# Expert rows gathered in channel quarters and turned on VectorE; copies of the last weights pinned in SP's queue

## The chip, the cores and the metric

One core of one Trainium2 chip runs the whole program. The metric is the device time of one execution in microseconds (us); for the kernel before it is the median of three runs. A profile is one further execution, taken by the hardware profiler.

The engines are called as the profile calls them: PE is TensorE (matrix products; PEld is its weight load), DVE is VectorE, ACT is ScalarE, POOL is GpSimd, and SP is SyncE, which here only issues transfers. Each engine works through its own queue in order and waits on semaphores for the others.

## The reference

The input is x of 4 rows (batches) x 512 tokens x 512 channels, in float32. Two layers are computed, each with a gate ahead of its mixer and a gate ahead of its feed-forward part:

```python
x = x + L0_attn(L0_cond(x, f, f, ...))    # a state-space mixer (Mamba-2)
x = x + L0_ffn(L0_cond2(x, f, f, ...))    # mixture of 8 experts, top 2
x = x + L1_attn(L1_cond(x, f, f, ...))    # causal attention, 16 heads, 4 key/value groups
x = x + L1_ffn(L1_cond2(x, f, f, ...))    # gated feed-forward part, 1408 wide
```

The part that the change touches is the mixture of experts:

```python
logits = x @ gate_w.T + gate_b
top_vals, top_idx = jax.lax.top_k(logits, 2)
routing = softmax(top_vals)
for e in range(8):
    h = x @ w1[e].T + b1[e]                     # 512 -> 1024
    x_glu, x_lin = h[:, 0::2], h[:, 1::2]
    y = x_glu * sigmoid(1.702 * x_glu) * (x_lin + 1.0)
    ye = y @ w2[e].T + b2[e]                    # 512 -> 512
    out = out + ye * sum(routing * (top_idx == e))
```

## The kernel before

**Stages.** The program is unrolled; its stages overlap where the data allow it. From the start to about 650 us the four rows go through the state-space mixer; from 654 to about 1130 us the expert blocks run, the first of them between the last tiles of the mixer; from about 1131 to 1985 us comes attention, 64 heads (4 groups x 4 rows x 4 heads); then the last feed-forward part. A generator (`make_gates`, L352) is advanced a step at a time inside all of these and makes the gates of later parts, mostly on VectorE and ScalarE, with transfers on SP's queue.

**Order of the work.** The source gives an order, and a planner lays every engine's instructions out in advance: among those that its model holds ready it takes the one that the source has first. So an instruction without a wait can stand much earlier in a queue than in the source. `after(*engines)` (L88) pins what is traced in it behind the last instruction that the source has given to those engines so far.

**The experts.** Each token goes to two of eight experts. The 4096 token places are sorted by expert into blocks of 128 (class `Experts`, L709). There are 39 block numbers; 37 (`ALWAYS`) are always run, the last two only where the routing needs them. The first 17 (`NEARLY`) hold tokens of the first three rows done and are ordered by a first routing table (`order_blocks(0, NEARLY)`, called at L1433); the other 22 by a second one (L1525), after the last row is routed. A table is made by small products on PE and small operations on VectorE (L648 to L707): `use` says which block numbers are in use, `rank` puts them in order (a product with the constant `tri_lt`, L663 or L672), `of` is the one-hot form of that order, and the products at L689 and L690 pick from `toks` the token places of every block and from `v_e` its expert. The results are `idx_h` (which row of `rows_h` each of the 128 lanes takes), `idx_o` (where its result goes) and `eb` (the expert).

`rows_h` lies in device memory, 2048 tokens x 512 channels. A block goes through these steps, one call of `round` (L864) per block, with three blocks in different steps at a time:

- `fetch` (L766): one indirect transfer from GpSimd's queue gathers 128 rows of 2 KB into `hb`, token by partition. It is asked for three blocks ahead; `hb` has three buffers.
- `flip` (L776): four 128x128 transposes on PE (L782) bring channels onto the partitions, and one copy on ScalarE (L784) takes the result from PSUM to `hT`, which has two buffers.
- `first_half` (L806): products with the two halves of w1 (L811 and L822, 4 products each, which the profile counts double), the bias and the gate on VectorE (L816, L826, L828, L829), the tanh on ScalarE. The result is `u`.
- `finish` (L832): four more transposes on PE (L835) and a scaled copy on ScalarE (L837) into `yT`.
- `down` (L840): products with w2 (L844), the bias on VectorE (L849), and an indirect transfer that scatters the rows into `rows_o` (L850).

The weights come over SP's queue (`load_w1` L742, `load_w2` L754) and are loaded only where the expert in the slot changes. From block 17 on there are two slots.

**Attention.** For each head, `scores` (L1626) makes the softmax, turns it in 32x32 blocks on VectorE (L1653, the operation that the change also uses), writes it to device memory from GpSimd's queue (L1661) and reads it back as `pT` on SP's queue (L1678, `collect`); `context` (L1682) multiplies it with the values (L1703), about a head later than the load is issued. Between the heads, SP's queue carries the gates' transfers (L240, L247, L249, L344) and group weights (L1466).

**Copies of the last weights.** `gateT`, `upT` and `downT` of the last feed-forward part are copied within device memory, 2816 KB each, by SP (L1763), to be loaded from there at L1834 to L1839. The source has these three transfers in attention, at the first heads of rows 0 to 2 of group 2, and they wait for nothing. In the profile they are issued at 51.0, 56.9 and 57.4 us.

Of the kernel before, what the change touches and what calls it, by code (L numbers as in the profile page):

```python
# [10 lines left out]
F32 = mybir.dt.float32  # L11
# [35 lines left out]
HPG = HEADS // GROUPS  # L47
SCALE = KVC ** -0.5
# [35 lines left out]
def block_kernel(ctx: ExitStack, tc: tile.TileContext, a: dict, out: bass.AP):  # L84
# [61 lines left out]
    def ps_tp(name):  # L146
        return ps.tile([P, 512], F32, tag="tp", name=name, bufs=2)
# [263 lines left out]
    def gated(l, b, xb, pool, part=slice(0, T), **kw):  # L411
# [25 lines left out]
    tri_lt = rt.tile([P, P], F32, name="tri_lt")  # L437
    nc.gpsimd.affine_select(out=tri_lt, in_=ones, compare_op=ALU.is_gt, fill=0.0, base=0,
                            pattern=[[1, P]], channel_multiplier=-1)

# [36 lines left out]
    v_lo = rt.tile([P, 1], F32, name="v_lo")  # L477
    v_e = rt.tile([P, 1], F32, name="v_e")
# [48 lines left out]
    def route(lg, b, fine, pool, **kw):  # L527
# [25 lines left out]
        nc.tensor.matmul(pc[:, :n], lhsT=tri_lt, rhs=mm_, start=True, stop=True)  # L553
# [89 lines left out]
    idx_h = rt.tile([P, NBLK], I32, name="idx_h")  # L643
# [4 lines left out]
    def order_blocks(lo, hi):  # L648

        n = hi - lo  # L650
        cv = rt.tile([P, 1], F32, tag="cv", name="cv")
# [10 lines left out]
        if lo == 0:  # L662
            nc.tensor.matmul(pi[:, P : P + 1], lhsT=tri_lt, rhs=use, start=True, stop=True)  # L663
            nc.vector.tensor_copy(rank, pi[:, P : P + 1])
        else:
# [6 lines left out]
            nc.tensor.matmul(pi[:, P : P + 2], lhsT=tri_lt, rhs=two, start=True, stop=True)  # L672
# [9 lines left out]
            )  # L682
        if lo == 0:
            nc.vector.scalar_tensor_tensor(taken, rank, float(n), use, ALU.is_lt, ALU.mult)
# [7 lines left out]
        gf = tmp.tile([P, NBLK], F32, tag="th", name="gf")  # L692
        nc.vector.tensor_scalar(gf[:, :n], pi[:, :n], NROW - 2.0, None, ALU.add)
        nc.vector.tensor_copy(idx_h[:, lo:hi], gf[:, :n])
        low = tmp.tile([P, NBLK], I32, tag="th", name="low")
        nc.vector.tensor_scalar(
            low[:, :n], idx_h[:, lo:hi], T - 1, (B - 1) * T, ALU.bitwise_and, ALU.bitwise_xor
        )
        nc.vector.tensor_scalar(
            idx_h[:, lo:hi], idx_h[:, lo:hi], 1, (B - 1) * T,  # L700
            ALU.logical_shift_right, ALU.bitwise_and,
        )
        nc.vector.tensor_tensor(idx_h[:, lo:hi], idx_h[:, lo:hi], low[:, :n], ALU.bitwise_xor)
# [5 lines left out]
    class Experts:  # L709
# [56 lines left out]
        def fetch(self, i):  # L766
            if i >= self.known or i in self.hb:
                return
            hb = self.sm.tile([P, C], F32, tag="hb", name="hb", bufs=3)
            nc.gpsimd.indirect_dma_start(  # L770
                out=hb, out_offset=None, in_=rows_h[: (B if i >= NEARLY else B - 1) * T, :],
# [1219 lines left out]
```

## Time and profile before

| what | value |
|---|---|
| runs | 2265.02, 2266.19 and 2270.69 us; median 2266.19 |
| the profiled execution's own time | 2262.92 us |
| its span, from the first to the last instruction | 2260.90 us |
| mean granted PE clock | 0.983 |
| busy: PE, PEld, DVE, ACT, POOL | 2123.0, 1219.8, 1524.8, 971.5, 418.4 us |
| DMA: bytes moved, mean rate | 357.38 MB, 158 GB/s |
| expert stage, 655 to 1130 us: PE, DVE, ACT, POOL busy | 452.2, 260.3, 141.7, 92.1 of 475 us |
| attention, 1131 to 1985 us: PE, DVE, ACT, POOL busy | 824.1, 574.7, 328.1, 136.0 of 854 us |

How to read the lines. A group of instructions is given by its source line, engine and operation, what it writes and reads (partitions x elements, type), how often, then busy us and the mean ns of one, then the idle time of the engine just ahead of it and what ended that. In an answer by time the first two columns are start and duration in us, and the brackets hold the idle time ahead. An answer by windows has, for each stretch, its length, the busy us of each engine (with the number of instructions), the granted PE clock, the busy share of the 16 DMA engines and their GB/s. Products on PE are pipelined, so their durations overlap; what one costs is read from start to start.

### The profile page before, as it was taken

What the parts mean: (1) busy time and instruction counts of PE and PEld (TensorE: products, weight loads), DVE (VectorE), ACT (ScalarE), POOL (GpSimd) and SP (SyncE); (2) the same over time, 40 slices, a digit from 0 to 9 for tenths busy, and PEclk for the clock granted to TensorE, in tenths of its full rate; (3) what the DMA queues carried; (4) which work ended last, traced back from release to release, by engine and by line L of the source; (5) the groups of instructions that cost most, each with busy time, mean ns of one, the idle gap of its engine ahead of it and who ended that gap; (6) DMA issues with size and microseconds to landing.
All of it is one profiled execution on the core that took longest, in us unless ns stands there. A gap on an engine that the chain in (4) does not pass through costs nothing.

```text
span 2260.9 us, 23897 instructions
## 1 busy us (share of the span) xinstructions
PE 2123.0 (94%) x7528; PEld 1219.8 (54%) x7528; DVE 1524.8 (67%) x3040; ACT 971.5 (43%) x1901; POOL 418.4 (19%) x558
## 2 busy tenths in 40 slices
PE   2879999999999999999989999999999999999998
PEld 1545565555655444444444555545555555568887
DVE  8698989989643665566577767677767765465332
ACT  4476676766732234333154433333334333243221
POOL 4023242321331111211211111111111111100000
PEclk9889999999999999999989999999999999999999
DMA  7542241531523548978666555455545464441100
GB/s 261 174 141 75 95 166 66 169 111 63 193 71 135 192 159 297 352 261 292 210 238 206 177 181 168 140 164 185 169 151 164 147 196 133 148 158 38 38 19 20
DMA packets 112455, 357.38 MB, mean 158 GB/s; under 512 B 14595, under 2 KB 23171, under 8 KB 102915
## 3 DMA queue, kind: packets, MB, share of 16 engines
q1 hardware_dynamic: 87584, 277.26, 36.1%
q0 software_dynamic: 22432, 74.34, 11.0%
q10 hardware_dynamic: 2304, 4.20, 0.5%
q8 instruction: 62, 1.02, 0.2%
q14 instruction: 73, 0.57, 0.1%
HBM read 337.91 MB, written 108.00 MB: 197 GB/s over the span
## 4 chain that ended last, share of the span: by engine, by line
PE 36%; DVE 9%; DMA 2%; ACT 2%; issue 1%; SPq 0%; DVEq 0%; ACTq 0%
PE pd L1718 9%; PE pq L1615 5%; PE pctx L1703 3%; PE psc L1637 3%; PE pk L1593 3%; PE pv L1601 3%; PE pfo L1821 2%; PE pfo L1820 2%; PE pfg L1820 2%; PE pfg L1821 2%; PE pfu L1821 2%; PE pfu L1820 2%; DVE turned L1653 2%; DVE nmax L1642 2%; DMA pT<-turned 1%; DVE pr L1649 1%
## 5 line engine op out<-in xcount | busy, mean ns | idle before, releaser
L1661 POOL DMA_DIRECT2D turned<-turned x248 | 135.2, 552 | 701.2 <-DVE turned L1653 399.0
L1615 PE MATMUL pq<-h,wq 128*128 128x512 f32 x512 | 230.9, 593 | 2.2 <-DVE h L404 1.7
L1718 PE MATMUL pd<-cx,wd 128*128 128x512 f32 x512 | 224.0, 593 | 1.9 <-ACT cx L1711 1.6
L128 ACT ACTIVATE pr<-psc,nmax 128x128 f32<-128x128 f32 (+3 forms) x256 | 134.6, 526 | 166.1 <-DVE nmax L1642 165.4
L1048 PE MATMUL pc<-h,wxb 128*128 128x512 f32 x320 | 148.5, 620 | 42.8 <-DVE h L1307 38.9
L1640 DVE TENSOR_TENSOR psc<-psc,mask 128x128 f32<-128x128 f32 x256 | 70.7, 284 | 144.3 <-PE psc L1637 144.3
L1637 PE MATMUL psc<-kT,qT 128*128 128x128 f32 (+3 forms) x512 | 156.3, 442 | 12.0 <-ACT pr L128 12.0
L1718 PEld LDWEIGHTS pd<-cx,wd 128*128 128x128 f32 x512 | 95.6, 190 | 118.5 <-issue 108.1
L1703 PE MATMUL pctx<-pT,v 128*128 128x512 f32 (+3 forms) x512 | 149.7, 434 | 9.9 <-DMA pT<-turned 9.6
L1703 PEld LDWEIGHTS pctx<-pT,v 128*128 128x128 f32 x512 | 96.6, 190 | 90.2 <-issue 61.1
L1615 PEld LDWEIGHTS pq<-h,wq 128*128 128x128 f32 x512 | 92.6, 190 | 96.3 <-issue 90.8
L811 PE MATMUL pg<-w,hT 128*128 128x512 f32 x296 | 136.6, 603 | 6.8 <-ACT hT L784 6.8
L844 PE MATMUL po<-w,yT 128*128 128x512 f32 x296 | 135.9, 600 | 6.2 <-ACT yT L837 6.2
L822 PE MATMUL pn<-w,hT 128*128 128x512 f32 x296 | 133.4, 593 | 0.0
L1048 PEld LDWEIGHTS pc<-h,wxb 128*128 128x128 f32 x320 | 61.9, 198 | 115.8 <-issue 73.8
L1642 DVE TENSOR_REDUCE nmax<-psc 128x1 f32<-128x128 f32 (+3 forms) x256 | 122.7, 482 | 2.1
L1637 PEld LDWEIGHTS psc<-kT,qT 128*128 128x128 f32 x512 | 85.9, 192 | 70.5 <-ACT pr L128 26.9
L1726 DVE TENSOR_TENSOR xr<-xr,pd 128x512 f32<-128x512 f32 x64 | 43.5, 680 | 117.7 <-PE pd L1718 117.7
L1653 DVE STREAM_TRANSPOSE turned<-pr 128x128 f32<-128x128 f32 x248 | 120.7, 498 | 1.8
L1119 PE MATMUL pz<-wzt,h 128*128 128x512 f32 x256 | 115.2, 599 | 0.3 <-ACT st L1220 0.3
L1267 PE MATMUL po<-wot,yT 128*128 128x512 f32 x256 | 114.2, 600 | 0.0
L811 PEld LDWEIGHTS pg<-w,hT 128*128 128x128 f32 x296 | 56.2, 194 | 75.9 <-issue 66.3
(343 smaller groups left out, 4172.9 us busy)
## 6 DMA issues: line engine op xcount, KB each, us to landing
w<-in_w1x SPq DMA_DIRECT2D x76, 1024.0 KB
turned<-turned POOLq DMA_DIRECT2D x248, 208.0 KB, 4.0
pT<-turned SPq DMA_DIRECT2D x62, 832.0 KB
w<-in_w2x SPq DMA_DIRECT2D x38, 1024.0 KB
wb<-in_b1x SPq DMA_DIRECT2D x38, 512.0 KB
lm<-cs SPq DMA_DIRECT2D x32, 512.0 KB
kt<-in_fT SPq DMA_DIRECT2D x62, 256.0 KB
ek<-ek SPq DMA_DIRECT2D x62, 256.0 KB
```

Source lines behind the costliest of these rows:

```text
L811: nc.tensor.matmul(pg, lhsT=hT[:, k, :], rhs=self.w1[s][0][:, k, :], start=(k == 0), stop=(k == NC - 1))
L844: nc.tensor.matmul(po, lhsT=yT[:, j, :], rhs=self.w2[s][:, j, :], start=(j == 0), stop=(j == NI - 1))
L1048: nc.tensor.matmul(pc, lhsT=wxb[:, k, m * P : (m + 1) * P], rhs=h[:, k, :], start=(k == 0), stop=(k == NC - 1),)
L1615: nc.tensor.matmul(pq, lhsT=u.wq[:, k, i * KVC : (i + 1) * KVC], rhs=u.h[:, k, :], start=(k == 0), stop=(k == NC - 1),)
L1637: nc.tensor.matmul(psc[:, :n], lhsT=qT[:, qi * P : n], rhs=u.kT[:, :n], start=True, stop=True)
L1642: nc.vector.tensor_reduce(nmax, psc[:, :n], AX.X, ALU.max, negate=True)
L1653: nc.vector.transpose(blocks[:, :, 3 * qi : 4 * qi + 1, :].rearrange("p c k j -> p k c j"), pr)
L1661: nc.gpsimd.dma_start(out=d[:, :, r].rearrange("c i s -> i c s"), in_=blocks[r * SQ : (r + 1) * SQ].rearrange("i c k j -> i c (k j)"),)
L1703: nc.tensor.matmul(pctx[:, kj * P :].rearrange("p (q r j) -> p q r j", r=QUAD, j=SQ), lhsT=u.v[:, kj, :], rhs=pT[:, :, 4 * kj : 10 + kj : ...
L1718: nc.tensor.matmul(po, lhsT=dense_w[u.g][:, i, m * P : (m + 1) * P], rhs=u.ctxT[i], start=(i == 0), stop=(i == HPG - 1),)
L1820: nc.tensor.matmul(out_, lhsT=w, rhs=xs[0], start=first_, stop=False)
L1821: nc.tensor.matmul(out_, lhsT=w, rhs=xs[1], start=False, stop=last_)
```

## The change

It has four parts.

1. **Gather by quarters.** `rows_h` is read as rows of 128 channels, four to a token. `idx_h` gets four columns per block. `fetch` issues four indirect transfers per block instead of one, each with 128 rows of 512 bytes. Partition 32q + i of part r takes channel quarter q of token 32r + i of the block.
2. **Turn on VectorE.** `flip` becomes one `nc.vector.transpose` of 128x512, which turns each 32x32 block; its output is `hT` with the channels in another order, and w1 is laid out to that order on the host (`by_quad`). PE's four transposes and ScalarE's copy are gone.
3. **The routing table.** In each `order_blocks` a tile `wide` (128x512, made from `toks` by one copy on VectorE) takes part in four more products with `of`; the index operations work on four times the columns, and one more combines in `quarter`, which is made there too, by an iota on GpSimd and an operation on VectorE. `tri_lt`, a constant made at the start, is gone: the counts use `tri_gt`, and the ranks `tri_le` with `use` subtracted.
4. **The copies.** The three transfers of L1763 are put into `after(nc.sync)`.

```diff
@@ -45,6 +45,8 @@
 
 HEADS, GROUPS, KVC = 16, 4, 128
 HPG = HEADS // GROUPS
+SQ = 32
+QUAD = P // SQ
 SCALE = KVC ** -0.5
 MASKED = -1.0e30
 
@@ -434,10 +436,6 @@
     nc.gpsimd.affine_select(out=before, in_=before, compare_op=ALU.is_gt, fill=0.0, base=0,
                             pattern=[[1, E], [-1, E]], channel_multiplier=0)
 
-    tri_lt = rt.tile([P, P], F32, name="tri_lt")
-    nc.gpsimd.affine_select(out=tri_lt, in_=ones, compare_op=ALU.is_gt, fill=0.0, base=0,
-                            pattern=[[1, P]], channel_multiplier=-1)
-
     sel = rt.tile([P, E], F32, name="sel")
     nc.gpsimd.affine_select(out=sel, in_=ones[:, :E], compare_op=ALU.is_ge, fill=0.0, base=0,
                             pattern=[[-NQ, E]], channel_multiplier=1)
@@ -474,8 +472,8 @@
     e_nq = count("e_nq", [[NQ, E]])
     v_id = count("v_id", [[1, 1]], 1)
 
-    v_lo = rt.tile([P, 1], F32, name="v_lo")
-    v_e = rt.tile([P, 1], F32, name="v_e")
+    v_both = rt.tile([P, 2], F32, name="v_both")
+    v_lo, v_e = v_both[:, 0:1], v_both[:, 1:2]
     jk = rt.tile([P, E], F32, name="jk")
     nc.vector.tensor_tensor(jk, sel, e_nq, ALU.mult)
     nc.vector.tensor_reduce(v_e, jk, AX.X, ALU.add)
@@ -550,7 +548,7 @@
             yield
         pc = ps_tp("pcnt")
         mm_ = m.rearrange("p t e -> p (t e)")
-        nc.tensor.matmul(pc[:, :n], lhsT=tri_lt, rhs=mm_, start=True, stop=True)
+        nc.tensor.matmul(pc[:, :n], lhsT=tri_gt, rhs=mm_, start=True, stop=True)
         nc.tensor.matmul(pc[:, n : 2 * n], lhsT=ones, rhs=mm_, start=True, stop=True)
         for t in range(NT):
             bt = b * NT + t
@@ -640,7 +638,8 @@
 
 
     taken = rt.tile([P, 1], F32, name="taken")
-    idx_h = rt.tile([P, NBLK], I32, name="idx_h")
+    idx_h = rt.tile([P, QUAD, NBLK], I32, name="idx_h")
+    quarter = rt.tile([P, 1], I32, name="quarter")
     idx_o = rt.tile([P, NBLK], I32, name="idx_o")
     eb = rt.tile([1, NBLK + 1], I32, name="eb")
     in_use = eb[:, NBLK:]
@@ -648,6 +647,12 @@
     def order_blocks(lo, hi):
 
         n = hi - lo
+        if lo == 0:
+            with after(nc.gpsimd, nc.vector):
+                nc.gpsimd.iota(quarter, pattern=[[1, 1]], base=0, channel_multiplier=1)
+                nc.vector.tensor_scalar(
+                    quarter, quarter, 5, QUAD * (B - 1) * T, ALU.logical_shift_right, ALU.bitwise_xor
+                )
         cv = rt.tile([P, 1], F32, tag="cv", name="cv")
         nc.vector.tensor_tensor(jk, sel, cnt[:, (N2 if lo else N2 - NT), :], ALU.mult)
         nc.vector.tensor_reduce(cv, jk, AX.X, ALU.add)
@@ -660,8 +665,8 @@
         pi = ps_tp("pidx")
         rank = rt.tile([P, 1], F32, tag="vrank", name="vrank")
         if lo == 0:
-            nc.tensor.matmul(pi[:, P : P + 1], lhsT=tri_lt, rhs=use, start=True, stop=True)
-            nc.vector.tensor_copy(rank, pi[:, P : P + 1])
+            nc.tensor.matmul(pi[:, P : P + 1], lhsT=tri_le, rhs=use, start=True, stop=True)
+            nc.vector.tensor_tensor(rank, pi[:, P : P + 1], use, ALU.subtract)
         else:
 
             two = rt.tile([P, 2], F32, tag="two", name="two")
@@ -669,7 +674,7 @@
             nc.vector.tensor_reduce(rank, jk, AX.X, ALU.add)
             nc.vector.tensor_scalar(two[:, 0:1], v_lo, rank, use, ALU.is_lt, ALU.mult)
             nc.vector.tensor_tensor(two[:, 1:2], use, two[:, 0:1], ALU.subtract)
-            nc.tensor.matmul(pi[:, P : P + 2], lhsT=tri_lt, rhs=two, start=True, stop=True)
+            nc.tensor.matmul(pi[:, P : P + 2], lhsT=tri_le, rhs=two, start=True, stop=True)
             nc.tensor.matmul(pi[:, P + 2 : P + 3], lhsT=ones, rhs=two[:, 0:1], start=True, stop=True)
             nc.tensor.matmul(pi[0:1, P + 3 : P + 4], lhsT=ones[:, 0:1], rhs=use, start=True, stop=True)
             nc.vector.tensor_copy(in_use, pi[0:1, P + 3 : P + 4])
@@ -680,6 +685,7 @@
             nc.vector.scalar_tensor_tensor(
                 rank, pi[:, P : P + 1], two[:, 0:1], rank, ALU.mult, ALU.add
             )
+            nc.vector.tensor_tensor(rank, rank, use, ALU.subtract)
         if lo == 0:
             nc.vector.scalar_tensor_tensor(taken, rank, float(n), use, ALU.is_lt, ALU.mult)
         of = tmp.tile([P, NBLK], F32, tag="th", name="of")
@@ -689,18 +695,36 @@
         nc.tensor.matmul(pi[:, :n], lhsT=toks, rhs=of[:, :n], start=True, stop=True)
         nc.tensor.matmul(pi[0:1, 2 * P : 2 * P + n], lhsT=v_e, rhs=of[:, :n], start=True, stop=True)
 
-        gf = tmp.tile([P, NBLK], F32, tag="th", name="gf")
-        nc.vector.tensor_scalar(gf[:, :n], pi[:, :n], NROW - 2.0, None, ALU.add)
-        nc.vector.tensor_copy(idx_h[:, lo:hi], gf[:, :n])
-        low = tmp.tile([P, NBLK], I32, tag="th", name="low")
+
+        wide = tmp.tile([P, QUAD, QUAD, SQ], F32, tag="th", name="wide")
+        nc.vector.tensor_copy(
+            wide,
+            toks.rearrange("p (r j) -> p r j", r=QUAD).unsqueeze(2).to_broadcast([P, QUAD, QUAD, SQ]),
+        )
+        for r in range(QUAD):
+            nc.tensor.matmul(
+                pi[:, 3 * P + r * n : 3 * P + (r + 1) * n],
+                lhsT=wide[:, r].rearrange("p q j -> p (q j)"),
+                rhs=of[:, :n], start=True, stop=True,
+            )
+        ih = idx_h[:, :, lo:hi]
+        gf = tmp.tile([P, QUAD, n], F32, tag="th", name="gf")
         nc.vector.tensor_scalar(
-            low[:, :n], idx_h[:, lo:hi], T - 1, (B - 1) * T, ALU.bitwise_and, ALU.bitwise_xor
+            gf, pi[:, 3 * P : 3 * P + QUAD * n].rearrange("p (r n) -> p r n", r=QUAD),
+            NROW - 2.0, None, ALU.add,
+        )
+        nc.vector.tensor_copy(ih, gf)
+        low = tmp.tile([P, QUAD, n], I32, tag="th", name="low")
+        nc.vector.tensor_scalar(
+            low, ih, 2, QUAD * (T - 1), ALU.logical_shift_left, ALU.bitwise_and
         )
         nc.vector.tensor_scalar(
-            idx_h[:, lo:hi], idx_h[:, lo:hi], 1, (B - 1) * T,
-            ALU.logical_shift_right, ALU.bitwise_and,
+            ih, ih, 1, QUAD * (B - 1) * T, ALU.logical_shift_left, ALU.bitwise_and
         )
-        nc.vector.tensor_tensor(idx_h[:, lo:hi], idx_h[:, lo:hi], low[:, :n], ALU.bitwise_xor)
+        nc.vector.tensor_tensor(ih, ih, low, ALU.bitwise_xor)
+        nc.vector.tensor_tensor(
+            ih, ih, quarter.unsqueeze(2).to_broadcast([P, QUAD, n]), ALU.bitwise_xor
+        )
         ef = tmp.tile([1, NBLK], F32, tag="th", name="ef")
         nc.vector.tensor_scalar(ef[:, :n], pi[0:1, 2 * P : 2 * P + n], E - 1.0, None, ALU.add)
         nc.vector.tensor_copy(eb[:, lo:hi], ef[:, :n])
@@ -766,22 +790,25 @@
         def fetch(self, i):
             if i >= self.known or i in self.hb:
                 return
-            hb = self.sm.tile([P, C], F32, tag="hb", name="hb", bufs=3)
-            nc.gpsimd.indirect_dma_start(
-                out=hb, out_offset=None, in_=rows_h[: (B if i >= NEARLY else B - 1) * T, :],
-                in_offset=bass.IndirectOffsetOnAxis(ap=idx_h[:, i : i + 1], axis=0),
-            )
+            hb = self.sm.tile([P, QUAD, NC * SQ], F32, tag="hb", name="hb", bufs=3)
+            quarters = rows_h[: (B if i >= NEARLY else B - 1) * T, :].rearrange(
+                "r (q c) -> (r q) c", q=QUAD
+            )
+            for r in range(QUAD):
+                nc.gpsimd.indirect_dma_start(
+                    out=hb[:, r, :], out_offset=None, in_=quarters,
+                    in_offset=bass.IndirectOffsetOnAxis(ap=idx_h[:, r, i : i + 1], axis=0),
+                )
             self.hb[i] = hb
 
         def flip(self, i):
             if i in self.hT or i not in self.hb:
                 return
             hb = self.hb[i]
-            pt = ps_tp("pfl")
-            for k in range(NC):
-                nc.tensor.transpose(pt[:, k * P : (k + 1) * P], hb[:, k * P : (k + 1) * P], ident)
             hT = self.sm.tile([P, NC, P], F32, tag="hT", name="hT", bufs=2)
-            nc.scalar.copy(hT.rearrange("p k t -> p (k t)"), pt)
+            nc.vector.transpose(
+                hT.rearrange("p k (r j) -> p r k j", r=QUAD), hb.rearrange("p r c -> p (r c)")
+            )
             self.hT[i] = hT
 
         def weights(self, i, early=False):
@@ -1568,8 +1595,7 @@
             )
             return wd
 
-        SQ, SLOTS = 32, 13
-        QUAD = P // SQ
+        SLOTS = 13
         turned = [mp.tile([P, QUAD, SLOTS, SQ], F32, name=f"turned{i}") for i in range(2)]
         for blocks in turned:
             for lo, hi in ((1, 3), (5, 6)):
@@ -1760,7 +1786,8 @@
                 combine(b + 1)
             if g == 2 and i == 0 and b < 3:
                 to, name = ((ffg_d, "gateT"), (ffu_d, "upT"), (ffd_d, "downT"))[b]
-                nc.sync.dma_start(out=to, in_=a[name])
+                with after(nc.sync):
+                    nc.sync.dma_start(out=to, in_=a[name])
             if g and b == 0 and i == 3:
                 dense_w[g] = load_dense(g)
             if n + 1 < len(heads_):
@@ -1949,7 +1976,8 @@
         "gate_b": n["L0_ffn_gate_b"],
     }
     by_part = lambda v: v.reshape(E, -1, P, v.shape[-1]).swapaxes(1, 2)
-    w1x = np.stack([by_part(t(w1[:, i::2, :])) for i in range(2)], 2)
+    by_quad = lambda v: v.reshape(E, QUAD, NC, SQ, -1).swapaxes(2, 3).reshape(E, P, NC, -1)
+    w1x = np.stack([by_quad(t(w1[:, i::2, :])) for i in range(2)], 2)
     got = {
         "cols": np.concatenate([cols[k] for k, _ in _COLS], 1),
         "rows": np.concatenate([np.asarray(rows[k]) for k, _ in _ROWS]),
```

## The prediction

> **What bounds the kernel now.** I read the engines' shares first, then the slices, then the stage that the change touches, and there the waits and the instructions in order of time.
>
> ```profile
> PE 2123.0 (94%) x7528; PEld 1219.8 (54%) x7528; DVE 1524.8 (67%) x3040; ACT 971.5 (43%) x1901; POOL 418.4 (19%) x558
> ...
> PE   2879999999999999999989999999999999999998
> ...
> DMA  7542241531523548978666555455545464441100
> ```
>
> TensorE is full from the fourth slice on, so an instruction taken off its queue is worth its whole duration unless something else is about to end last. The expert blocks run from 654 to 1130 us. There the answer by windows (columns: stretch, length, busy us of PE, PEld, DVE, ACT, POOL, granted clock, DMA share, GB/s) reads:
>
> ```profile
> 840.00:880.00 40.00, 37.96 (x110) 17.76 (x109) 24.90 (x31) 15.73 (x21) 6.06 (x6) 1.00 0.80 274
> ...
> 920.00:960.00 40.00, 36.72 (x100) 17.18 (x99) 20.94 (x29) 13.49 (x18) 7.03 (x6) 0.96 1.00 373
> ...
> 1000.00:1040.00 40.00, 38.66 (x115) 18.80 (x114) 28.00 (x34) 13.89 (x21) 7.90 (x7) 1.00 0.76 273
> 1040.00:1080.00 40.00, 40.00 (x114) 19.00 (x113) 26.04 (x32) 11.02 (x17) 6.25 (x6) 1.00 0.69 241
> ```
>
> PE has 37 to 40 of each 40 us, VectorE at most 28, GpSimd 8. Only the DMA engines come close, and fill one window (share 1.00). So PE bounds this stage, with the weight stream just behind it. VectorE, ScalarE and GpSimd have room.
>
> **Removed: the TensorE flip.** Each of 37 blocks has four transposes (L782) and one copy out of PSUM on ScalarE (L784); the groups give busy us, mean ns of one, and the idle time before them.
>
> ```profile
> L782 PE MATMUL pfl<-ident,hb 128*128 128x128 f32 x148 | 23.2, 281 | 3.0 <-DMA hb<-rows_h,idx_h 3.0
> ```
>
> ```profile
> L784 ACT COPY hT<-pfl 128x512 f32<-128x512 f32 x37 | 21.5, 581 | 40.1 <-PE pfl L782 40.1
> ```
>
> In order of time (start, duration, what):
>
> ```profile
> 741.05 0.60 PE L782 MATMUL pfl<-ident,hb 128*128 128x128 f32 x4
> 741.49 3.60 PE L822 MATMUL pn<-w,hT 128*128 128x512 f32 x8
> ```
>
> The rows overlap by pipelining, so the cost is from start to start: 741.49 - 741.05 = 0.44 us per block; other blocks read the same. The first two flips stand in the wait for the first gather and are counted there; the other 35 give 35 x 0.435 = **-15.2 us**.
>
> The copy on ScalarE costs only where PE waits for it: three waits of PE for hT, 6.8 us in all. The longest is 4.18 us at 800.6; the product behind it then took 6.01 instead of 3.60 us (granted clock 0.93 in 800 to 840), so 9.2 us hang on it. Without the copy that product starts at once, but the next transposes need u (L829), which ends at 802.5 because ScalarE's tanh is late too; it would gain only the half us that the copy held it up. So about 4.5 us of that stall go, and little of the others: **-5** (bounds -9.2 and 0).
>
> **Added per block: four gathers and a VectorE transpose.** A gather is 0.94 to 1.48 us on GpSimd, 1.27 from start to start:
>
> ```profile
> 654.05 1.24 POOL L770 DMA_INDIRECT hb<-rows_h,idx_h  x1 [7.32 <-DVE eb L706]
> 655.59 0.97 POOL L770 DMA_INDIRECT hb<-rows_h,idx_h  x1 [0.30 <-issue]
> 656.86 0.95 POOL L770 DMA_INDIRECT hb<-rows_h,idx_h  x1 [0.30 <-issue]
> ```
>
> Four take 5.1 us where one took 1.3; with the scatter of the results (1.3) GpSimd has 6.4 us of work in a round of 11 to 12 us. Block i+3 is asked for when block i is turned, over two rounds (22 us) ahead; 5.1 plus 4.5 us to landing (median) fit in. The bytes stay the same, but rows shrink from 2 KB to 512 B. The packet records have 28.9 ns for a 512-byte packet, and 187 ns for two 2 KB rows: per block 512 x 28.9 / 16 = 0.92 us of all engines instead of 64 x 187 / 16 = 0.75, some 0.2 us, hidden except where DMA is full.
>
> The transpose has an exact row, the attention's own:
>
> ```profile
> L1653 DVE STREAM_TRANSPOSE turned<-pr 128x512 f32<-128x512 f32 x62 | 43.7, 704 | 1.1
> ```
>
> 37 x 0.704 = 26 us on VectorE, 0.70 in a round that uses some 8 of 12 us. It waits for four gathers; queued behind it on VectorE are the bias additions, gates and scans, and PE's next transposes wait for u. PE waits for u 0.7 us in the whole stage now. I take **+1** (0 to +5).
>
> The Trainium skill has a rule against this ("SBUF — State Buffer", "SBUF: two separate sides"): while VectorE runs a two-port operation, GpSimd cannot write descriptors, and a transfer of 620 ns took 3100. By that, 148 gathers 2.5 us longer each would cost 370 us of GpSimd, more than the stage has left, and the gathers would set the pace. The trace shows gathers of at most 1.48 us beside a busy VectorE; it does show 128x1 operations on GpSimd (L1247) of 0.34 to, in the mean, 1.26 us. No gather row shows the rule's price.
>
> **First table (651 to 662 us), fully exposed.** PE now waits 2.71 us for the first gather and starts the first product at 661.94, after two flips and eight transposes of the mixer (L1258). After the change come `wide` (0.5 to 0.7; nearest rows L1649 and L404 at 128x512: 476 and 697 ns), four more pairs of products (0.22 each from start to start, by L689 to L690) and two more small VectorE operations (0.18), partly beside other work: indices 1.3 us later. The fourth gather starts 3 x 1.27 = 3.8 us after the first. The turn is 0.70 instead of 1.08 (PE) + 0.59 (ScalarE). First operand: 659.5 + 1.3 + 3.8 - 1.0 = 663.6, product at 663.7: +1.8. The clock was at half from 655 to 662 (a flip 1.08 instead of 0.60); if that lasts 3.4 us longer at half speed, one or two such pieces add 1.7 or 3.4. Bounds 0 and +5.2; **+3.5**. `quarter` falls into GpSimd's idle 7.3 us: nothing.
>
> **Second table (772 to 778 us).** Its blocks are due 80 us later, so only PE's queue counts: 4 x 0.22 = 0.9, and a short wait for `wide`, as PE waits 1.14 for `of` (L686) today: **+1.2** (0.9 to 1.6).
>
> **Weight stream.** Faster rounds ask for weights sooner. In the window at share 1.00 PE already waits 3.28 us, put down to yT, which had long been there. About four rounds cannot shrink, and the smaller rows add 0.2 each to a few more: **+2** (0 to +9: all 20 rounds from 840 to 1080).
>
> **The late copies.** Three transfers of 2816 KB between HBM tensors are issued at 51.0, 56.9 and 57.4 us and occupy the DMA engines until 82 (9.8 us each). At that time only one wait for a DMA shows (VectorE, 0.8 us), so their going gains 0 to 0.8. Behind the change each stands on SP's queue ahead of attention's loads of pT. The packet records give each load's landing; it lands 17 to 29 us before its use for two heads of four, 7 to 9 for the third, and about 0.5 to 3 for the fourth:
>
> ```profile
> 1594.98 0.37 SPq L1678 DMA_DIRECT2D pT<-turned  x1
> ```
>
> ```profile
> 1601.45 2.39 PE L1703 MATMUL pctx<-pT,v 128*128 128x512 f32 x8 [2.55 <-DMA pT<-turned]
> ```
>
> A copy straight before the third load costs PE 9.8 - 7.4 = 2.4 us, before the fourth 9.3, before the others nothing: -0.8 to +28 for the three. `after(nc.sync)` pins them behind the last gate or pT transfer of the previous head, mostly ahead of a load with room: **+2**.
>
> **Sum**: -15.2 - 5 + 1 + 3.5 + 1.2 + 2 + 2 = -10.5. The profiled execution took 2262.92 us (span 2260.90 and 2.02 around it): 2252.4. The median of the runs shown is 2266.19, 3.3 above it; forecast for the median: 2255.7, or **2256 us**. All favourable ends (-15.2 - 9.2 + 0.9 - 0.8 = -24.3) give 2242; the unfavourable ones, with copies at 7: -15.2 + 5 + 5.2 + 1.6 + 9 + 7 = +12.6, 2279.
>
> **Rivals.** *No gain, 2266*: the weight stream holds the 20 rounds from 840 to 1080 at their length (+8.7 instead of +2, no gain from the copy on ScalarE): -10.5 + 6.7 + 5 = +1.2. For it: DMA share 0.69 to 1.00 there, half of all blocks. Against: PE fills those windows, and share 1.00 occurs in one.
>
> *Slower, 2282*: the copies land on the fourth head's load, which has 0.5 us to spare (PE waits 2.55 there today): 3 x 9.3 = 28 us instead of 2, so -10.5 + 26 = +15. It eats the whole gain from 4.2 us per copy on. For it: SP's queue is in order and the transfers behind a copy wait. Against: only one load in four is that tight.
>
> *It does not do what it says*: the copies stay early; then 2254.
>
> **Chances.** Forecast 0.62 (faster 0.56, same 0.06), no gain 0.22 (0.04, 0.16, slower 0.02), slower 0.16 (0.13, same 0.03). Bounded by 0.3% (6.8 us, about what a measurement of this kernel can tell from no change): faster 0.60, same 0.25, slower 0.15. Range: from the favourable end, 2242, up to 2278, where most of the slower rival is left out.
>
> **What would show it.** Right: no L782 or L784 rows; 148 gathers of about 1 us; 37 transposes of 0.70; rounds 0.44 us shorter except in one window; the first product near 664; no waits of PE for pT beyond 3 us around 1560 to 1690. Wrong: gathers of 2 us or more, PE waiting for the transpose, or the copies in front of a tight pT load. I hold the order of all other instructions to be unchanged; since it is planned anew, stalls may move elsewhere, and that is the largest unknown.

## The result, and the profile after

The changed kernel takes 2286.43 us (median of 6 runs, 2282.31 to 2287.86) where the kernel before takes 2265.61 beside it: a ratio of 1.0079, interval 1.0063 to 1.0095. It is 20.8 us slower; the forecast's sum had it 10.5 faster. The profiled execution took 2287.86 us (span 2286.0, granted clock 0.974 instead of 0.983).

The page after, engines' shares and slices as before:

```profile
PE 2131.2 (93%) x7396; PEld 1216.1 (53%) x7396; DVE 1546.0 (68%) x3083; ACT 951.8 (42%) x1864; POOL 545.3 (24%) x669
...
PE   2879999999987999999989999999999999999998
...
DMA  6142341432513457987667555456845464431100
```

PE is busy 8 us longer than before, VectorE 21 and GpSimd 127. And PE's twelfth and thirteenth slices (629 to 743 us), full before, have fallen to 8 and 7. The windows (stretch, length, busy us of PE, PEld, DVE, ACT, POOL, granted clock, DMA share, GB/s) give the place, and two windows of the later blocks for comparison:

```profile
680.00:720.00 40.00, 26.94 (x64) 12.08 (x63) 8.85 (x15) 3.31 (x6) 19.91 (x27) 0.83 0.29 92
...
920.00:960.00 40.00, 40.00 (x103) 18.27 (x102) 28.60 (x38) 12.79 (x17) 19.56 (x19) 1.00 1.00 361
1000.00:1040.00 40.00, 37.77 (x98) 17.11 (x97) 27.68 (x37) 12.56 (x17) 21.64 (x18) 1.00 0.72 258
```

From 680 to 720 us PE is busy 26.9 us of 40, at a clock of 0.83, while GpSimd works 19.9. Further on PE has its 38 to 40 us again. The two new operations, by groups:

```profile
L809 DVE STREAM_TRANSPOSE hT<-hb 128x512 f32<-128x512 f32 x37 | 25.9, 701 | 10.1 <-DMA hb<-rows_h,idx_h 10.1
```

```profile
L798 POOL DMA_INDIRECT hb<-rows_h,idx_h x148 | 172.1, 1163 | 158.0 <-DVE hT L809 107.6 <-issue 35.0 <-DVE idx_h L725 8.2
```

The turn takes the forecast 0.70 us. A gather takes 1.16 us in the mean and 2.0 at most, so no gather row shows the price of 3100 ns that the prediction weighed.

**Round by round.** The interval from one block's first product (L811, now L838) to the next block's is the measure of the blocks. The table has the rounds that differ, for the kernels that are told of below; the last two rows are the sum of 36 intervals and the half-clock time within them.

| round | before | after | after again (e9) | one pin (e1) | gates pinned: changed (e14) | before (e16) | mixture (e15) |
|---|---|---|---|---|---|---|---|
| 0 | 7.7 | 10.3 | 9.5 | 9.2 | 10.3 | 7.8 | 9.2 |
| 1 | 18.6 | **33.4** | **33.2** | 18.6 | 18.6 | 18.6 | 18.6 |
| 8 | 13.2 | 18.0 | 17.9 | 14.6 | 18.0 | 13.2 | 14.3 |
| 9 | 15.5 | 10.7 | 10.7 | 10.7 | 10.7 | 11.2 | 11.2 |
| 10 | 13.6 | 16.5 | 16.4 | 17.8 | 16.0 | 12.4 | 12.4 |
| 14 | 12.2 | 15.8 | 16.9 | 15.8 | 15.8 | 13.2 | 11.7 |
| 22 to 24, each | 11.2 | 10.7 | 10.7 | 10.7 | 10.7 | 11.2 | 10.7 |
| 25 | 12.8 | 13.2 | 13.2 | 13.2 | 10.7 | 11.2 | 10.7 |
| 29 | 12.8 | 14.9 | 14.9 | 14.9 | 10.7 | 11.2 | 10.7 |
| all 36 | 448.4 | 460.8 | 459.4 | 445.0 | 434.7 | 432.5 | 425.8 |
| half clock | 10.2 | 39.2 | 37.6 | 19.9 | 18.7 | 0.2 | 3.0 |

So in the profiled run the blocks lost 12.4 us: 2.6 in the first round, 14.8 in the second, and five later rounds (8, 10, 14, 25, 29) got 13.9 longer; the other 29 got 18.9 shorter in sum. Two further losses lie outside the blocks: 9.0 us before the first table, and 4.4 in the last feed-forward part. The 9.0, 0.3 at the first table, the 12.4, about -0.9 from the last block to the last part and the 4.4 add up, within rounding, to the 25.1 between the spans.

**The second round.** PE in order of time:

```profile
671.28 6.19 PE L838 MATMUL pg<-w,hT 128*128 128x512 f32 x8 [6.34 <-DVE hT L809]
...
681.60 3.60 PE L838 MATMUL pg<-w,hT 128*128 128x512 f32 x8
685.03 0.60 PE L862 MATMUL pyt<-ident,u 128*128 128x128 f32 x4
698.69 5.28 PE L871 MATMUL po<-w,yT 128*128 128x512 f32 x6 [13.06 <-ACT yT L864]
```

The transposes of the first block's `u`, which stand in this round, are recorded at 685.03, and the product that needs their result starts at 698.69: 13 us without work, put down to yT. Behind it the clock is at half (5.28 us for six products, 2.84 before). ScalarE in that time:

```profile
679.39 1.05 ACT L1286 COPY yT<-pyt 128x512 f32<-128x512 f32 x2
698.04 0.60 ACT L864 ACTIVATE yT<-pyt 128x512 f32<-128x512 f32 x1 [17.61 <-remote]
```

It makes yT at 698.04, and the answer names no engine of this core that would have held it. VectorE resumes at the same moment, with a product that is recorded as done at 685.2:

```profile
697.99 0.69 DVE L843 TENSOR_TENSOR g<-pg,wb 128x512 f32<-128x512 f32 x1 [1.51 <-remote]
```

The longer wait (13.06 us, 0.25 before) makes 12.8 us, the half clock 2.4, the flip that is gone saves 0.4: together the 14.8 of this round. GpSimd, meanwhile:

```profile
663.91 1.25 POOL L798 DMA_INDIRECT hb<-rows_h,idx_h  x1 [8.16 <-DVE idx_h L725]
665.45 0.97 POOL L798 DMA_INDIRECT hb<-rows_h,idx_h  x1 [0.30 <-issue]
...
693.22 0.94 POOL L798 DMA_INDIRECT hb<-rows_h,idx_h  x1 [0.30 <-issue]
694.17 1.28 POOL L1241 TENSOR_TENSOR y<-y,zs 128x512 f32<-128x512 f32 x1
```

24 gathers stand in one row, a start every 1.25 us, for 30 us. The mixer's next y (ready at 686.7) follows behind them, and VectorE waits 9.6 us for the norm's rv that comes after y. PE does not wait for this y here: all of its loss in the round is the wait for yT and the clock behind it. Before, five gathers stood there. And SP's issues in the same stretch:

```profile
677.50 0.07 SPq L768 DMA_DIRECT2D w<-in_w1x  x1
680.29 0.70 SPq L779 DMA_DIRECT2D w<-in_w2x  x1
685.26 0.70 SPq L780 DMA_DIRECT2D wb<-in_b2x  x1
691.59 0.69 SPq L768 DMA_DIRECT2D w<-in_w1x  x1
```

They take 0.70 us instead of 0.07; the register operations between them, 0.04 to 0.06 us elsewhere, are recorded with 0.70 too, from 678.8 to 697.9. In the trace's semaphore records the counter that ScalarE waits for (PE's) rises at 685.29 and then only at 697.96, although the transposes were issued by 685.4. The last landing recorded in that stretch is at 695.4; 2.5 us later everything goes on.

### The profile page after: what moved, and what is told of

Its sections match the earlier page's. It is cut to its first block, busy times and chain, and to the rows that moved or that the text cites. A ratio compares the mean times of both kernels' runs of the same rounds, so it can differ in the third digit from the quotient of the medians.

```text
span 2286.0 us, 23765 instructions
## 1 busy us (share of the span) xinstructions
PE 2131.2 (93%) x7396; PEld 1216.1 (53%) x7396; DVE 1546.0 (68%) x3083; ACT 951.8 (42%) x1864; POOL 545.3 (24%) x669
## 4 chain that ended last, share of the span: by engine, by line
PE 35%; DVE 9%; DMA 3%; ACT 2%; issue 1%; SPq 0%; POOL 0%; DVEq 0%; ACTq 0%
PE pd L1744 8%; PE pq L1641 5%; PE pctx L1729 3%; PE pv L1627 2%; PE pk L1619 2%; PE psc L1663 2%; PE pfg L1848 2%; PE pfu L1848 2%; PE pfo L1848 2%; PE pfg L1847 2%; PE pfo L1847 2%; PE pfu L1847 2%; DVE turned L1679 2%; DVE nmax L1668 1%; DMA pT<-turned 1%; DVE pr L1675 1%
## 5 line engine op out<-in xcount | busy, mean ns | idle before, releaser
L798 POOL DMA_INDIRECT hb<-rows_h,idx_h x148 | 172.1, 1163 | 158.0 <-DVE hT L809 107.6
L871 PE MATMUL po<-w,yT 128*128 128x512 f32 x296 | 144.6, 632 | 20.1 <-ACT yT L864 19.8
L838 PE MATMUL pg<-w,hT 128*128 128x512 f32 x296 | 137.6, 607 | 6.4 <-DVE hT L809 6.3
```

The costliest lines, as they stand in the source:

```text
L798: nc.gpsimd.indirect_dma_start(out=hb[:, r, :], out_offset=None, in_=quarters, in_offset=bass.IndirectOffsetOnAxis(ap=idx_h[:, r, i : i + ...
L838: nc.tensor.matmul(pg, lhsT=hT[:, k, :], rhs=self.w1[s][0][:, k, :], start=(k == 0), stop=(k == NC - 1))
L871: nc.tensor.matmul(po, lhsT=yT[:, j, :], rhs=self.w2[s][:, j, :], start=(j == 0), stop=(j == NI - 1))
```

## The experiments

Time depends on the clock that the chip grants, which is not the same in all runs of one kernel. In 92 runs of the kernel before, taken beside the experiments, the time lies between 2259.6 and 2282.2 us at clocks of 0.984 to 0.974, along a line of 1.9 us per 0.001 (2268.8 at 0.980; scatter 1.6). "Against the line" below is the mean distance to it at the run's own clock. A change that makes PE wait lowers its own clock, so this distance leaves out what a kernel loses by that.

**The changed kernel again**, as it is.

> The changed kernel once more, beside the others on one chip. In 21 runs of the kernel before the time fell with the granted clock, 2.0 us per 0.001; read at equal clock the changed kernel stood 8 us above it, and the other 12 us of its 20.8 came with a clock of 0.975 against 0.98. If that split holds: 6 to 10 us above the line of the kernel before at its own clock, and 12 to 14 us of them between the second and third block. If the clock was only chance: the same clock as the runs of before here, total 2274 to 2280. If the change itself lowers the clock: 0.974 to 0.977, total 2282 to 2288.

2287.55 us against 2267.12 (ratio 1.0078, 1.0053 to 1.0102), clock 0.975 in the mean, 8.8 us above the line. The second round takes 33.2 us again. Before the first table this profile is only 1.6 us late instead of 9.0. So the 20 us repeat, and with them the low clock: the change lowers it. Of half clock 38 to 39 us fall into the blocks, 28 more than before; half of that over 2286 us is 0.006 of mean clock. The 9.0 us of the mixer are another matter (next but one).

**One pin: gathers behind what GpSimd was given before.**

```
-            self.fetch(i + self.LOOK)
+            with after(nc.gpsimd):
+                self.fetch(i + self.LOOK)
```

> The changed kernel with one pin: each round's gathers stand in GpSimd's queue behind whatever the source has given GpSimd so far. Ahead of the mixer's next y then stand 16 gathers instead of 24. Burst theory (the 33.4 us between the first products of the second and third block, 18.5 before the change, come from the gathers that stand back to back at the start): 20 to 25 us there, total 2272 to 2278. Rival (the VectorE transpose or the copies lose the time): still 33 us there, total 2283 to 2289. The 9 us that the mixer lost before the blocks stay in both.

2276.29 us against 2270.41 (1.0037, 1.0009 to 1.0066), 0.5 above the line. The second round is back at 18.6 us, with PE's longest wait for yT 0.7 us. SP's issues in that stretch:

```profile
678.07 0.07 SPq L779 DMA_DIRECT2D w<-in_w2x  x1
...
681.07 0.07 SPq L768 DMA_DIRECT2D w<-in_w1x  x1
```

They take 0.07 again. Burst theory holds: 16 gathers in a row instead of 24 took back 14.8 us of that round.

**Only the new constants**, in the kernel before (tri_lt removed, v_lo and v_e in one tile, ranks by tri_le).

> The kernel before with only the new constants: no tri_lt, v_lo and v_e in one tile, the ranks by tri_le. Clock theory (the mixer's 9 us before the blocks come from a start that is shifted by about 1 us, which moves PE's waits against the windows in which the clock is granted): the blocks start 8 to 10 us later than in the kernel before, extra half-clock pieces between 285 and 490 us, total 2273 to 2277. Rival (they come from the blocks' new order further on, or from the copies that are gone at the start): no shift, total 2263 to 2269.

2271.47 against 2270.41 (1.0025, 1.0002 to 1.0049). The blocks do start 9.0 us later in its profile. But they start 7.3 later in the next experiment, whose start is otherwise untouched, and 1.6 in the repeat of the changed kernel, whose start is changed. So my clock theory falls: these microseconds come with the run, not with the new constants. The kernel is yet 5.7 us above the line, and its profile shows where: 4.4 us are lost in the last feed-forward part, as in the changed kernel.

**Only the late copies**, in the kernel before (the pin `after(nc.sync)`).

> The kernel before with only the three copies pinned late. The prediction's term: +2 us (bounds -0.8 and +28), total 2264 to 2270. If the copies take bandwidth from pT's loads: 2275 to 2294. If their going from the start shifts the mixer against the clock's windows: blocks start 3 to 10 us later, total 2269 to 2276.

2270.98 against 2270.41 (1.0005, 0.9988 to 1.0021), 0.5 above the line, no drift in the last part. The copies cost nothing that can be measured.

**Two tiles again**: the pinned kernel (e1) with v_lo and v_e in two tiles.

```
-    v_both = rt.tile([P, 2], F32, name="v_both")
-    v_lo, v_e = v_both[:, 0:1], v_both[:, 1:2]
+    v_lo = rt.tile([P, 1], F32, name="v_lo")
+    v_e = rt.tile([P, 1], F32, name="v_e")
```

> The pinned kernel with v_lo and v_e in two tiles again, as before the change. That moves all later tiles up by 32 bytes, the last part's weights from an address of 0 to one of 32 in 64. Placement theory (the last part's drift of 4.4 us comes from where its weights lie: its products 7 ns slower each): drift gone, 0.227 us per product again, total 4 to 5 us less than the pinned kernel at equal clock, so 3 to 5 us below the kernel before. Rival (the drift comes from the instruction stream or from the copies): still 4 us in the last part.

2270.67 against 2267.12 (1.0016, 0.9994 to 1.0037), 1.3 us below the line. Its time against the pinned kernel can't be read to 4 us (0.5 above the line there, 2 us of uncertainty). Its second round took 22.3 us in the profile, 3.7 more than in e1, with 16 gathers in a row in both. The last part can be read from the profile: 0 us of drift instead of 4.4. One group of its products, before, after and here (count, busy us, mean ns):

```profile
L1821 PE MATMUL pfg<-h_lo,ffg 128*128 128x512 f32 x172 | 67.0, 389 | 0.0
```

```profile
L1848 PE MATMUL pfg<-h_lo,ffg 128*128 128x512 f32 x172 | 68.1, 396 | 0.0
```

```profile
L1849 PE MATMUL pfg<-h_lo,ffg 128*128 128x512 f32 x172 | 67.0, 389 | 0.0
```

From start to start these and the pfu products take 0.227 us before and here, 0.234 after; the 690 of them make 4.5 us. The third kind, pfo, takes 0.233 in all. What differs for these products is where the weights lie in a partition: in the built programs, pfg's at byte 62432 before and here (32 in 64), at 62400 in the changed kernel and at 61888 with only the new constants (both 0 in 64); the moving operands lie where they lay. The next kernel adds a case: its weights lie 64 bytes lower than before (62368), and pfg and pfu take 0.229, but pfo 0.227. So 0.227 occurs where weights and moving operand begin at the same place in 128 bytes (both at 96 for pfg and pfu before and here, both at 32 for pfo in the next kernel), and 0.229 to 0.234 where they do not. That is read from three placements, and none was chosen to test this rule.

**Four gathers, but TensorE's flip**: the kernel before, its gather split into four of 512-byte rows, token by partition (with the new constants, and four small VectorE operations per table for the indices).

> The kernel before with four gathers of a quarter row each per block and TensorE's flip as it was (the new constants too, and four small VectorE operations per table for the quarters' indices). 20 gathers then stand back to back ahead of the mixer's next y. Burst theory: 5 to 12 us more than in the kernel before between the second and third block, nothing gained in the rounds, total 8 to 14 us above the line of the kernel before at equal clock. Rival (the VectorE transpose makes the loss): 18.5 us there as before, total within 4 us of that line.

2289.29 against 2267.12 (1.0076, 1.0052 to 1.0101), 12.1 above the line. Rounds 0, 1 and 3 take 10.6, 22.5 and 28.5 us (7.7, 18.6 and 22.6 before), the others nearly what they took. In round 1 PE waits 2.45 us for a yT (the mixer's this time) that ScalarE makes at 690.16, again held by no engine of this core. In round 3 the loss has another path: `rv` stands behind gathers on GpSimd until 717.8, VectorE waits 6.8 us for it with `lg` behind, and PE waits for `lg` and then runs at half clock:

```profile
720.70 1.12 PE L515 MATMUL pht<-ident,h_last 128*128 128x128 f32 x4 [2.90 <-DVE lg L506]
721.61 5.13 PE L817 MATMUL pg<-w,hT 128*128 128x512 f32 x6
```

The loss comes without VectorE's transpose, and the new constants alone (above) left these rounds as they were: it is the gathers that make it. The converse, VectorE's transpose behind one gather (e4), gave no result, so the transpose without the split gathers is not measured.

**The transpose twice**, in the pinned kernel (e1).

> The pinned kernel with each block transpose done twice, into the same tile: 26 us more on VectorE. The prediction's term (+1 us for 26 us, VectorE has room): 0 to 3 us above the pinned kernel. Rival (the rounds beside which the gates are made are bound by VectorE and ScalarE): 0.7 us in each of the 10 or so rounds that wait for u or yT, 5 to 10 us above.

2284.16 against 2267.12 (1.0059, 1.0034 to 1.0083), 6.3 above the line, so 5.8 more than once (2.8 of uncertainty). 26 us on VectorE are not free: PE's waits in the gates' rounds grow from 2.83 to 3.30 us, and half clock from 19.9 to 28.0 us.

**One VectorE operation less**: u in one operation, without the linear bias.

> The pinned kernel with two tiles; the bias of the linear half of w1 is left out, so that u takes one VectorE operation instead of two: 0.7 us per round less on VectorE, about what the block transpose adds. Theory (the rounds beside which the gates are made are bound by VectorE, so that its 26 us cost 5 to 8): 4 to 8 us less than the pinned kernel with two tiles. Rival (VectorE has room, +1): 0 to 2 us less.

2281.01 against 2267.73 (1.0079, 1.0048 to 1.0111): slower by 10 than with the bias, at a clock of 0.974. Both theories fall. VectorE's sum alone is not the bound; the shorter rounds were planned into another order, in which yT stands behind all of the gates' operations on ScalarE, and PE waits 4.47 us three times. That led to the next pair. The cause had been in view: ScalarE in round 29, before, and at the same place after:

```profile
1036.35 1.28 ACT L124 ACT_TABLE_LOAD   x1
1037.65 1.15 ACT L124 ACTIVATE rec<-rec,tiny 128x1024 f32<-128x1024 f32 x1
1038.70 0.58 ACT L837 ACTIVATE yT<-pyt 128x512 f32<-128x512 f32 x1
```

```profile
1057.09 1.15 ACT L318 ACTIVATE rec<-den,tiny 128x1024 f32<-128x1024 f32 x1 [0.76 <-DVE den L278]
1058.26 1.28 ACT L126 ACT_TABLE_LOAD   x1
1059.55 1.15 ACT L126 ACTIVATE rec<-rec,tiny 128x1024 f32<-128x1024 f32 x1
1060.61 0.58 ACT L864 ACTIVATE yT<-pyt 128x512 f32<-128x512 f32 x1
```

yT's copy (L837, L864) takes 0.58 us but stands behind two passes of the gates (`rec`; before the change the first one starts at 1035.18) and a table load, 3.5 us in all. PE reaches its product with w2 earlier now, by the flips it no longer does, and waits longer: 1.93 us from its last start before, 2.83 after. Then the product runs at half clock, 5.40 us instead of 3.70 (before and after):

```profile
1039.33 3.70 PE L844 MATMUL po<-w,yT 128*128 128x512 f32 x8 [1.34 <-ACT yT L837]
1061.24 5.40 PE L871 MATMUL po<-w,yT 128*128 128x512 f32 x8 [2.24 <-ACT yT L864]
```

The Trainium skill ("TensorE: Matmul & The Clock Gate", "Part 1: The HAM clock gate") has the clock fall to half after an idle window of some 3.4 us, on windows that do not start with the work. The lengths of the half-clock pieces agree: nearly all last 3.4, 6.8 or 10.2 us. The threshold does not: waits of 2.83 us, in which PE's records leave only some 2.2 us idle, halved the clock in 9 of 17 cases, so less than a whole idle window was enough. Waits for yT of 1.93 us (1.34 idle) did so in none of 8.

**Two blocks ahead instead of three**, in the pinned kernel with two tiles (`LOOK = 2`).

> The pinned kernel with two tiles, gathers asked for two blocks ahead instead of three: 12 gathers ahead of the mixer's next y instead of 16. Burst theory: 18.5 to 19 us between the second and third block, no half clock there, later rounds unchanged, 0 to 4 us less than with 16. Rival (two blocks are too short for four gathers and the turn): PE waits for hT in several rounds, 5 to 20 us more.

2273.90 against 2267.73 (1.0025, 1.0009 to 1.0041), 2.6 below the line. Round 1 takes 18.6 us, and PE waits for hT nowhere behind the first product: two blocks ahead are enough.

**The mixture**: 17 blocks as before the change, 20 by quarters and VectorE.

> A mixture: the 17 blocks of the first table as before the change (one gather of whole rows, TensorE's flip), the 20 of the second by quarters and VectorE; v_lo and v_e in two tiles. The first half of w1 lies in device memory in both layouts, and block 18 loads its weights unasked. Theory (the loss is made at the first table, by the gathers that crowd GpSimd; the second half gains 6 to 8 us as in the pinned kernel): blocks 0 to 16 as before, 6 to 8 us less from 17 to 36, no drift in the last part: 5 to 9 us below the line of the kernel before at equal clock. Rival (the gain of the later rounds is given back by the gates' work on VectorE and ScalarE or by the unasked weights): within 3 us of that line.

2270.18 against 2267.73 (1.0009, 0.9996 to 1.0023), 3.1 below the line. Rounds 1 to 7 are as before, but from 17 on only 6.5 us are gained: the gates' rounds (21, 25, 29) take 14.9, 13.2 and 14.9 us.

**The gates pinned on ScalarE too**, so that yT's copy goes first; in the changed kernel (e11) and in the kernel before.

```
-                    with after(nc.vector):
+                    with after(nc.vector, nc.scalar):
                         send()
                         pump(1 + moe.i % 2)
```

> The pinned kernel with two tiles and two blocks ahead, and one pin more: in the rounds without the mixer the gates' steps stand behind the round's own work on ScalarE too, not on VectorE alone, so that yT's copy goes ahead of Relu, Ln and Exp and their two table loads instead of between or behind them. Theory (the rounds' gain is lost because yT waits on ScalarE behind the gates; a longer wait then halves TensorE's clock): the waits of 2.83 us at the products with w2 go, intervals of 13 to 18 us become 11 to 13, 15 to 20 us less in the 36 rounds than in the kernel before (448.5), total 2252 to 2262. Rival (the gates themselves, VectorE's scans or the weights set the pace): the waits only move, 445 us as with the other pinned kernels, total 2268 to 2274.

> The kernel before with the same pin of the gates' steps and nothing else. By the theory the waits for yT go here too (1.93, 1.93 and 3.87 us, with less half clock behind them): 438 to 445 us in the 36 rounds, 3 to 9 us below the line of the kernel before at equal clock. The difference to the changed kernel with the pin is then what the flips are worth where nothing else waits: 13 to 18 us by the prediction's 35 x 0.435. Rival: no change against the kernel before.

The changed kernel with it takes 2262.04 us against 2270.75 (0.9965, 0.9946 to 0.9983), the kernel before with it 2252.25 (0.9912, 0.9890 to 0.9934). The order on ScalarE in the changed kernel is now:

```profile
1033.58 0.58 ACT L864 ACTIVATE yT<-pyt 128x512 f32<-128x512 f32 x1
1034.44 1.15 ACT L318 ACTIVATE rec<-den,tiny 128x1024 f32<-128x1024 f32 x1 [0.28 <-DVE den L278]
```

and rounds 25 and 29 take 10.7 us each; in the kernel before with the pin, 11.2. The pin is worth 18 us without the change, 13.5 against the line where I expected 3 to 9. And with the pin the changed kernel is 10 us slower than the unchanged one, where I expected it 13 to 18 faster. The two profiles say where: its last 19 rounds are 7.6 us shorter, its first 17 are 8.2 longer (2.6 in round 0, 4.8 in round 8, 3.6 in round 10), and 6.2 us lie ahead of the first table, where the times differ from run to run.

**The mixture with that pin**, and the kernel before with it once more beside it.

> The mixture (17 blocks by one gather and TensorE's flip, 20 by quarters and VectorE, two tiles, w1's first half in both layouts) with the gates pinned on ScalarE as well. If the loss lies in the first 17 blocks and the tables: blocks 0 to 7 as in the kernel before with the pin, 10.7 instead of 11.2 us from 17 on (19 x 0.45 = 8.6 less), 2 to 5 us lost at the second table: 3 to 7 us less than the kernel before with the pin, 2243 to 2251. If something else takes the gain back: within 2 us of the kernel before with the pin, or above it.

> The kernel before with the gates pinned, once more beside the mixture: 2248 to 2256 us, 434 us for the 36 rounds.

2247.23 us against 2270.51 for the mixture (0.9897, 0.9875 to 0.9918), 2250.68 for the kernel before with the pin (0.9911, 0.9889 to 0.9932). From round 17 on the mixture is 7.5 us shorter, near the 19 x 0.435 = 8.3 of the prediction's term; in the first 17 it loses 0.8. Their intervals overlap: 3.5 us in the median (16.7 against 12.2 below the line) lean to the mixture, and the profile says why, but the ratios alone do not separate the two. Either beats both kernels of this study.

## Why the prediction was wrong, point by point

- **The step that failed** is the hiding of the four gathers: "5.1 plus 4.5 us to landing (median) fit in". The cost of one was right (1.25 us from start to start). But at the first table there is no round yet: three blocks are asked for at once, and the planner put three more behind them. 24 x 1.25 = 30 us took the place of five gathers, some 6 us. In the later part of that row PE's results reached ScalarE and VectorE 12 us late, and the second round went from 18.6 to 33.4. I had asked whether the gathers come in time for their block, not what a long row of them does to the rest of the core. e1, with 16 in a row, takes the 14.8 us back; e5, with 20, loses time without the transpose, in one round by a late yT again and in another by what stands behind gathers on GpSimd (`rv`). That second path was missing from the prediction too.
- **The flip, -15.2**: right in kind and size where nothing else ends last: 0.44 us in each undisturbed round, 7.5 of 8.3 us in the last 19 rounds of e15. In the changed kernel 29 rounds gave 18.9 us, ScalarE's copy included.
- **And given back**: five rounds took 13.9 (4.8 at the second table and 2.9 in round 10, both below; 6.2 in rounds 14, 25 and 29). What is late next I asked only of the stall at 800.6, not of the rounds with the gates. The gates' operations on ScalarE end at a time of their own; what PE saves between them comes back as a wait, 2.83 instead of 1.93 us, and beyond that as half clock; with the gates pinned (e14) rounds 25 and 29 take 10.7. I had read 37 to 40 busy us of 40 as bound by PE in every round, while windows of 40 us average the round that waits with the three that do not.
- **ScalarE's copy, -5**: round 9 did lose 4.8 us, and round 10 gave 2.9 back. Net 1.9, within the bounds.
- **VectorE's turn, +1** (0 to 5): probably under-sized. Doubling it costs 5.8 (2.8 of uncertainty), about the upper bound; e12, with less work on VectorE and no gain, points to the planned order around it rather than to the sum of VectorE's time.
- **First table, +3.5**: 0.3 us of later first product (1.8 forecast) and 2.6 in the round behind, mostly half clock: 2.9.
- **Second table, +1.2**: 1.1 in e15, where the rest is as before; 4.8 in the changed kernel, as a wait of 2.7 us there halved the clock for 6.8; 1.4 in e1, where the same wait left the clock full.
- **Weight stream, +2**: PE's waits for weights are 0.3 us. **Late copies, +2**: 0.5 within 1.0. The slower rival came near by its number, 2282, and that was luck: its mechanism, the copies, cost nothing measurable.
- **Not in the sum at all**: the last part's 4.4 us. Constants and tables that take 32 bytes less moved the weights of a stage 1400 us later; nothing in the diff's lines points there.
- **What stays open**: why PE's signals and SP's operations are slow beside the long row of gathers. The semaphore and landing records thin out in the same stretch, and SP's records fall on steps of 0.70 us, some with a length of 0.01, so part of the picture may be the recording's; the lost time is in every run. And whether the change shifts the mixer's clock: its profiles are 9.0 and 1.6 us late there, the kernel before's with the pin 2.0 and 4.3. Over all profiles the kernels that split the first table's gathers are 1.6 to 14.0 late, the others 0 to 8.9: the ranges overlap.

## What to carry to other kernels

Before splitting a transfer that a computing engine issues, count the whole burst at the stage's start, read what stands behind it on that engine, and break the row up: a row of 24 cost 14.8 us here that 16 did not. An instruction taken off the busiest engine pays in the rounds where that engine ends last; look round by round, and find in the queue of the other engine what ends the waits of the rest, because putting that in order (18 us by one pin) can be worth more than the instruction. And a wait of some 3 us on TensorE can cost its length again, by the half clock behind it: 2.7 us at the second table were followed by 6.8 us at half clock, which is 3.4 lost.

## What the runs showed of the hardware

- Beside a long row of gathers (128 rows of 512 bytes each, one every 1.25 us) SP's register operations are recorded with 0.70 us instead of 0.04 to 0.06. In the profiles that show it, it holds from about 14 us after the row's first gather (18 at the latest) until 2 to 4 us after its last: 19 us with 24 gathers (both profiles of the changed kernel), 8 with 16 (e7, e8 and e12, but not at all in e1), 3 with 12 in e11 and not at all in e14. With 24, TensorE's completions reached ScalarE 12 us late.
- A gather occupies GpSimd for 0.95 us and the next starts 1.25 after it, with rows of 512 bytes as with 2 KB.
- Products of 128x512 took 0.227 us from start to start where weights and moving operand began at the same place in 128 bytes of a partition, and 0.229 to 0.234 where they did not (three placements of the weights).
- The mean granted clock of the kernel before varied from 0.974 to 0.984 over 92 runs, with 1.9 us per 0.001.
